# Two-layer transformer on one core: weights Hadamard-transformed by halves with sum and difference on leaving PSUM, and single-pass transposes of split keys and maxima

## The chip, the cores and the metric

The kernel runs on one core of a Trainium2 chip. The metric is the device time of one execution in microseconds (us), the median over several executions.

## The reference

The input x is 2 sequences of 1,024 rows of 256 numbers, all in float32. Two layers follow, each with attention and a feed-forward part that read the same normalised rows:

```python
xn = layernorm(x)
x = x + L0_attn(xn) + L0_ffn(xn)      # linear attention with elu+1; ternary weights
xn = layernorm(x)
x = x + L1_attn(xn) + L1_ffn(xn)      # softmax attention with rotary embedding; Hadamard FFN

# L1_ffn, with fwht the normalised Walsh-Hadamard transform over the last axis
h = fwht(xn * SU_ug) / 64
up, gate = h @ W_up.T * (Wscale_ug[:1024] * 64), h @ W_gate.T * (Wscale_ug[1024:] * 64)
y = fwht(silu(gate) * up * SU_dp) / 64
y = y @ W_down.T * (Wscale_dp * 64)
```

There are 16 heads of 16 numbers, and the inner width of the feed-forward parts is 1,024. The transforms act on the activations in the reference. The kernel moves them to the weights: it transforms the gate, up and down weights once and uses the transformed ("effective") weights in ordinary matrix products.

## The kernel before

Rows are kept in four chunks of 512. Products run on TensorE in float32, or, where operands are split into a high and a low part, in float32r (reduced float32), which TensorE takes in a single pass. PSUM is divided into two `pair` buffers for scores (two banks each), one bank `po` for attention outputs, and three `bank` buffers that everything else shares.

Up to about 290 us the kernel does layer 0 for the first sequence, the attention of layer 0 for the second, and a first search for maxima. From there on the softmax attention of layer 1 goes through eight units of four heads. A unit has 16 slots, and a slot has two halves. In each half TensorE makes a "burst": scores `scm` of the next unit, from which VectorE takes the maximum (`scores_max`, `peak`, L695), and scores `sce` of this unit minus their maxima, on which ScalarE takes the exponential (`weights_exp`, L740). In the first half TensorE then weighs the values (`weigh`, L748); in the second half it does other work that a planner hands out.

The order on the engines is written out by hand. Generators stand in the queue `filler` (the feed-forward part of layer 0, `hadamards`, `ffn1`), in `urgent` (`heads_of`, which makes the queries and keys of the next heads) and in `background` (`norm1` and `butterflies`). `slot` gives the filler its share, the work left (`left`) over the slots left (`to_fill`), and `fill` steps through the generators until their stated costs use the share up. A generator can also yield a mark: after SOON or FIRST it goes on after the burst of a first half, after SECOND after that of a second half (`go_on`). `fill` stops at FIRST and SECOND, and at SOON unless more than `LEAD` (0.85 us) of the share is unused. `background` is stepped once for each first half.

`hadamards` is

```python
yield from hadamard_down()            # ends with background.append(butterflies(wd1))
yield from hadamard_in("wgT1", "wA")
force(background)
yield from hadamard_in("wuT1", "wB")
```

`hadamard_in` transforms a weight of 256 x 1,024, held as two halves `raw[:, 0]` and `raw[:, 1]` of 128 rows. The 256-row transform is [[H, H], [H, -H]] with the 128-row matrix H (`hm`), so each of the two output halves is a sum of two products in PSUM; VectorE multiplies by the signs `su_ug` on the way out (L589). `butterflies` finishes the transform of the down weights in three levels of 1,024 columns, half on GpSimd (L614) and half on VectorE (L615), and then scales eight slices on VectorE (L619); its second buffer has the tag `wB`, which the effective up weights use afterwards. `force(background)` runs all that is left of `norm1(3)` and `butterflies` at once. `norm1` normalises a chunk (`norm_T`), transposes it and ends with the addition of the output bias to x on GpSimd (L438).

`heads_of` splits the rotated keys into a high and a low part (`split_k`), both written as float32r into `ks`; `lay_out` then transposes two groups of queries (float32, L475) and two of keys (L477) into a `bank` for each of eight row blocks. `put_peaks` transposes the negated maxima, also split into two float32r parts (`tops`), in four transposes (L719).

Of the kernel before, what the change touches and what calls it, by code (L numbers as in the profile page):

```python
# [20 lines left out]
P = 128  # L21
# [23 lines left out]
def tile_two_layers(ctx: ExitStack, tc: tile.TileContext, a: dict, out: bass.AP):  # L45
# [12 lines left out]
    def bank(name):  # L58
        return ps.tile([P, C], F32, tag="bank", name=name, bufs=3)
# [4 lines left out]
    def load(pool, name, view, shape, tag=None):  # L64
        tag, bufs = tag or (name, 1)
        t = pool.tile(list(shape), F32, tag=tag, name=name, bufs=bufs)
        nc.sync.dma_start(out=t, in_=view)
        return t
# [17 lines left out]

    ident = const.tile([P, P], F32, tag="ident", name="ident")
    make_identity(nc, ident)
    ones_r = const.tile([P, P], F32R, tag="ones_r", name="ones_r")
    nc.vector.tensor_scalar(ones_r, ident, 0.0, 1.0, ALU.mult, ALU.add)  # L90
    minus_half = const.tile([P, CT], F32, tag="minus_half", name="minus_half")
# [359 lines left out]
    def heads_of(b, gg, first=0, last=BT):  # L451

        if (b, gg) not in head_tiles:
            pool = late[0] if gg else at
            thk = pool.tile([P, 4, S], F32R, tag="qk_hi", name="qk_hi", bufs=1)
            tl = pool.tile([P, 2, S], F32R, tag="ql", name="ql", bufs=1)
            tv = pool.tile([P, BT, HH, VW], F32, tag="va", name="va", bufs=1)

            nc.gpsimd.memset(tv[:, :, :, HD:], 1.0)
            for i in range(2):  # L460
                g = 2 * gg + i
                qh[b, g], ql[b, g], kk[b, g] = thk[:, i, :], tl[:, i, :], thk[:, 2 + i, :]
                va[b, g] = tv[:, :, 4 * i : 4 * i + 4, :]
            head_tiles[b, gg] = thk, tl, tv
        thk, tl, tv = head_tiles[b, gg]
        half = HD // 2
        w3 = slice(gg * 3 * P, (gg + 1) * 3 * P)
        bias = qkvb[:, w3]

        def lay_out(i, rot, ks):  # L470
            cols = slice(i * P, (i + 1) * P)
            pt = bank("pt").rearrange("p (g n) -> p g n", g=4)
            for g in range(2):
                q4 = rot[:, 4 * g : 4 * g + 4, :, :].rearrange("p h s d -> p (h s d)")
                nc.tensor.transpose(pt[:, g, :], q4, ident)  # L475
                k4 = ks[:, 4 * g : 4 * g + 4, :, :].bitcast(F32).rearrange("p h s d -> p (h s d)")
                nc.tensor.transpose(pt[:, 2 + g, :], k4, ident)  # L477
            return cols, pt

        def take_out(cols, pt):  # L480
            nc.scalar.copy(thk[:, :, cols], pt)
            nc.vector.tensor_tensor(tl[:, :, cols], pt[:, 0:2, :], thk[:, 0:2, cols], ALU.subtract)

        def split_k(i):
            (rot,) = made[i]
            ks = at.tile([P, HH, 2, HD], F32R, tag="ks", name="ks")
            nc.scalar.copy(ks[:, :, 0, :], rot[:, HH:, 0, :])
            nc.gpsimd.tensor_tensor(ks[:, :, 1, :], rot[:, HH:, 1, :], ks[:, :, 0, :], ALU.subtract)
            made[i].append(ks)


        made = {}
        for i in range(first, last + 2):
            if i >= first + 2:
                cols, pt = lay_out(i - 2, *made.pop(i - 2))
                yield 4 * P * TR
                take_out(cols, pt)
            if i >= last:
                yield 0.0, LAST
                if i == last:  # L500
                    split_k(i - 1)
                    yield 0.0, PAIR
                continue
            c, j = divmod(b * BT + i, CT)
            pqkv = bank("pqkv")[:, 0 : 3 * P]
            for k in range(2):
                nc.tensor.matmul(  # L507
                    pqkv,
                    lhsT=xnT[c][:, k, j * P : (j + 1) * P],
                    rhs=wqkv[:, k, w3],  # L510
                    start=(k == 0),
                    stop=(k == 1),
                )
                if k == 0:
                    yield 3 * P * COL
            yield 3 * P * COL, LAST
            if i > first:
                split_k(i - 1)
            yield 0.0, FIRST
            qk = at.tile([P, 2 * HH, 2, half], F32, tag="qk", name="qk", bufs=1)  # L520
            nc.vector.tensor_add(qk.rearrange("p h t f -> p (h t f)"), pqkv[:, 0 : 2 * P], bias[:, 0 : 2 * P])
            nc.vector.tensor_add(
                tv[:, i, :, 0:HD],
                pqkv[:, 2 * P :].rearrange("p (h d) -> p h d", d=HD),
                bias[:, 2 * P :].rearrange("p (h d) -> p h d", d=HD),
            )
            cos, sin = (
                trig[:, i, s, :].unsqueeze(1).unsqueeze(1).to_broadcast([P, 2 * HH, 2, half]) for s in range(2)
            )
            qs = at.tile([P, 2 * HH, 2, half], F32, tag="qs", name="qs", bufs=1)  # L530
            nc.gpsimd.tensor_tensor(qs, qk, sin, ALU.mult)
            nc.gpsimd.tensor_tensor(qk, qk, cos, ALU.mult)

            rot = at.tile([P, 2 * HH, 2, HD], F32, tag="rot", name="rot")
            twice = [P, 2 * HH, 2, half]
            a0, a1, b0, b1 = (t[:, :, h, :].unsqueeze(2).to_broadcast(twice) for t in (qk, qs) for h in range(2))
            nc.gpsimd.tensor_tensor(rot[:, :, :, half:], a1, b0, ALU.add)
            yield 0.0, SECOND
            nc.vector.tensor_tensor(rot[:, :, :, 0:half], a0, b1, ALU.subtract)
            made[i] = [rot]  # L540
            yield 0.0, PAIR


    hm = load(const, "hadamard", a["hadamard"], [P, P])
    hneg = const.tile([P, P], F32, tag="hneg", name="hneg")
    nc.vector.tensor_scalar_mul(hneg, hm, -1.0)
    su_ug = load(const, "su_ug", a["su_ug"], [P, 2])
    su_dp = load(const, "su_dp", a["su_dp"], [P, NB])
    ws_dp = load_row(const, "ws_dp", D)

# [10 lines left out]
    def load_raw(count=2):  # L561
        for _ in range(count):
            if raws:
                name, n = raws.pop(0)
                raw = at.tile([P, 2, C], F32, tag="stage", name="raw", bufs=3)
                if name == "wdT1":
                    view = a[name].rearrange("(k p) n -> p k n", p=P)[:, 4 * n : 4 * n + 4, :]
                    nc.sync.dma_start(out=raw.rearrange("p a (b n) -> p (a b) n", b=2), in_=view)
                else:
                    view = a[name].rearrange("(k p) n -> p k n", p=P)[:, :, n * C : (n + 1) * C]  # L570
                    nc.sync.dma_start(out=raw, in_=view)
                loaded.append(raw)

    def hadamard_in(name, tag):
        eff = const.tile([P, 2, E], F32, tag=tag, name=f"eff_{name}")
        had[name] = eff
        for n in range(E // C):
            cols = slice(n * C, (n + 1) * C)
            raw = loaded.pop(0)
            for m in range(2):  # L580
                pw = bank("pw")
                for k, h in enumerate((hm, hneg if m else hm)):
                    nc.tensor.matmul(pw, lhsT=h, rhs=raw[:, k, :], start=(k == 0), stop=(k == 1))
                    if k == 0:
                        yield C * COL
                if m:
                    load_raw(1)
                yield C * COL, SOON
                nc.vector.tensor_scalar_mul(eff[:, m, cols], pw, su_ug[:, m : m + 1])  # L589
                yield 0.0  # L590

    def hadamard_down():
        wd1 = const.tile([P, NB, D], F32, tag="wC", name="wd1")
# [118 lines left out]
    def put_peaks(u, n):  # L712

        if n == 0:
            mx[u] = late[0].tile([P, S], F32R, tag="mx", name="mx")
        pt = bank("pt")
        for t in range(CT):
            top = tops[:, t, :, :].bitcast(F32).rearrange("p h d -> p (h d)")
            nc.tensor.transpose(pt[:, t * P : (t + 1) * P], top, ident)  # L719
        nc.scalar.copy(mx[u][:, n * C : (n + 1) * C], pt)  # L720
        left[0] -= CT * P * TR
        spent[0] += CT * P * TR

    def weights_of(u, i, p, sc):

# [140 lines left out]
    LEAD = 0.85  # L866
    ffn0_cost = 8 * NB * F * PASS + 2 * D * NB * 2 * PASS
    ffn1_cost = 48 * F * COL
    heads_cost = BT * (6 * P * COL + 4 * P * TR)
    norm_cost = 2 * CT * P * TR  # L870
    attention_cost = 2 * len(units) * norm_cost + NC * (norm_cost + CT * 2 * D * COL)

    with tc.manual_schedule(engines={PE}):

# [7 lines left out]
        def search(steps):  # L882
# [26 lines left out]
        filler += [*layer0[0:2], lambda: norm1(2), *layer0[2:4], lambda: norm1(3), hadamards()]  # L909
        filler += [ffn1(cc) for cc in range(8)]  # L910
        left[0] = (
            4 * ffn0_cost + 2 * norm_cost + 20 * C * COL + 8 * ffn1_cost + 3 * heads_cost + attention_cost
        )

    ordered[0] = True
# [125 lines left out]
```

## Time and profile before

| | |
|---|---|
| time, median of 3 runs | 970.14 us (968.78 to 972.83) |
| the profiled execution | 971.25 us, of which the span of the profile is 969.1 |
| mean granted TensorE clock | 0.974 |
| TensorE busy | 883.8 us, 91% of the span |
| VectorE, ScalarE, GpSimd busy | 586.2, 443.5, 215.4 us |
| transposes of keys (L477) and of maxima (L719) | 64 and 64 |
| matmul records of `pw` (all Hadamard products) | 40, between 400 and 441 us |

In the profile's lines a group is named by line, engine, operation and tiles (output<-inputs); then follow the count, the busy time in us and the mean duration in ns, and the idle time ahead of it with what ended it. In a timeline a line has the start, the length, the engine and the operation, and in brackets the idle time before it. A float32 product appears as two matmul records, a transpose or a float32r product as one.

### The profile page before, as it was taken

Reading aid. Unit: us, or ns where it says so; the run is one execution under the profiler, and the core shown is the slowest. Engines: PE = TensorE matmul, PEld = TensorE weight load, DVE = VectorE, ACT = ScalarE, POOL = GpSimd, SP = SyncE. Lnnn points to the kernel's source line nnn. Section 1 sums busy time; section 2 is a strip of 40 time slices with the busy share of each in tenths; the row PEclk is TensorE's granted clock in tenths of the full one; section 3 lists DMA queues with packets and bytes.
Section 4 is the critical chain, followed back from the end, with each engine's and each line's share of the span. In section 5 each row is a group of like instructions: output and inputs, shape, how many; then the busy total and the mean of one; then the engine's idle time right before and its main releaser. Section 6 shows DMA issues by size and latency. Waiting matters only on the chain.

```text
span 969.1 us, 14603 instructions
## 1 busy us (share of the span) xinstructions
PE 883.8 (91%) x6030; PEld 527.5 (54%) x6030; DVE 586.2 (60%) x975; ACT 443.5 (46%) x659; POOL 215.4 (22%) x287
## 2 busy tenths in 40 slices
PE   5778786878999999989999999999999999999987
PEld 2368674446555666434555555555555555555543
DVE  2744465478676687686775656567666665656311
ACT  5443435311454666334554434345444444444553
POOL 1634556510363233042420000045000000000000
PEclk9899898988899999999999999999999999999999
DMA  9100000000000001100000000000000000000000
GB/s 318 37 1 1 0 1 1 1 0 1 1 1 1 1 22 36 53 23 1 1 1 2 1 1 1 4 19 1 2 1 22 1 1 1 2 1 1 1 12 33
DMA packets 11249, 14.77 MB, mean 15 GB/s; under 512 B 1200, under 2 KB 8880, under 8 KB 11184
## 3 DMA queue, kind: packets, MB, share of 16 engines
q1 hardware_dynamic: 11184, 13.85, 4.3%
q8 instruction: 47, 0.77, 0.3%
q14 instruction: 18, 0.15, 0.0%
HBM read 11.75 MB, written 2.10 MB: 14 GB/s over the span
## 4 chain that ended last, share of the span: by engine, by line
PE 64%; DVE 23%; POOL 5%; issue 4%; ACT 3%; DMA 1%; SPq 0%; POOLq 0%; ACTq 0%; DVEq 0%
DVE peak L695 16%; PE scm L673 14%; PE pug L148 12%; PE sce L673 6%; PE py L171 6%; PE pqkv L507 4%; PE pug L96 4%; PE pkv L96 3%; PE py L96 2%; PE po L748 2%; POOL hid L385 2%; PE pq L96 1%; PE py L420 1%; PE sc L673 1%; ACT pr L740 1%
## 5 line engine op out<-in xcount | busy, mean ns | idle before, releaser
L740 ACT ACTIVATE pr<-sce 128x1024 f32<-128x1024 f32 x256 | 260.2, 1023 | 282.0 <-PE sce L673 281.8
L695 DVE TENSOR_REDUCE peak<-scm 128x2 f32<-128x1024 f32 x224 | 274.0, 1223 | 171.7 <-PE scm L673 170.6
L748 PE MATMUL po<-pr,va 128*17 128x512 f32 x1024 | 136.5, 602 | 0.0
L673 PE MATMUL scm<-qk_hi 32*128 32x512 f32 x448 | 112.2, 497 | 14.7 <-DVE peak L695 4.2
L673 PEld LDWEIGHTS scm<-qk_hi 32*128 32x128 f32 x448 | 41.7, 182 | 153.0 <-DVE peak L695 116.7
L673 PE MATMUL sce<-qk_hi 32*128 32x512 f32 x512 | 122.6, 497 | 2.6 <-ACT pr L740 1.8
L673 PE MATMUL sce<-mx,ones_r 32*128 32x512 f32 x512 | 97.1, 393 | 0.0
L673 PE MATMUL sce<-ql,qk_hi 32*128 32x512 f32 x512 | 97.0, 394 | 0.0
L709 POOL CAST tops<-nm 128x16 fp32r<-128x16 f32 x16 | 3.5, 219 | 388.6 <-DVE nm L698 388.5
L673 PE MATMUL scm<-qk_hi,ql 32*128 32x512 f32 x448 | 89.3, 395 | 0.0
L148 PE MATMUL pug<-xnT,eff_wgT 128*128 128x256 f32 x256 | 68.9, 391 | 0.1
L148 PE MATMUL pug<-xnT,eff_wuT 128*128 128x256 f32 x256 | 68.8, 383 | 0.0
L171 PE MATMUL py<-wd,hid 128*128 128x256 f32 x256 | 62.3, 388 | 0.0
L385 POOL TENSOR_TENSOR hid<-act,hid 128x256 fp32r<-128x256 f32 x64 | 46.8, 733 | 69.2 <-ACT hid L384 47.1
L171 PEld LDWEIGHTS py<-wd,hid 128*128 128x128 f32 x256 | 46.6, 190 | 16.2 <-issue 11.0
L158 ACT ACTIVATE act<-pug,ws_ug 128x256 f32<-128x256 f32 x64 | 30.3, 473 | 54.3 <-PE pug L148 54.3
L148 PEld LDWEIGHTS pug<-xnT,eff_wgT 128*128 128x128 f32 x256 | 46.0, 190 | 16.5 <-issue 10.3
L148 PEld LDWEIGHTS pug<-xnT,eff_wuT 128*128 128x128 f32 x256 | 47.8, 190 | 9.9 <-issue 3.3
L673 PEld LDWEIGHTS sce<-qk_hi 32*128 32x128 f32 x512 | 45.8, 182 | 11.9 <-ACT pr L740 8.2
L673 PEld LDWEIGHTS sce<-mx,ones_r 32*128 32x128 f32 x512 | 46.4, 184 | 10.5
L96 PE MATMUL pug<-xs,t_wuT 128*128 128x256 f32 x256 | 46.4, 304 | 4.7 <-DVE act L408 3.3
L507 PE MATMUL pqkv<-wqkvT,xnT 128*128 128x384 f32 x128 | 49.3, 506 | 0.9 <-DVE act L408 0.9
(157 smaller groups left out, 1349.0 us busy)
## 6 DMA issues: line engine op xcount, KB each, us to landing
x<-in_x SPq DMA_DIRECT2D x4, 512.0 KB, 7.7
out<-x SPq DMA_DIRECT2D x12, 128.0 KB, 1.7
both<-in_wuT SPq DMA_DIRECT2D x1, 1024.0 KB, 9.6
both<-in_wgT SPq DMA_DIRECT2D x1, 1024.0 KB, 11.7
wdT<-in_wdT SPq DMA_DIRECT2D x1, 1024.0 KB, 13.8
raw<-in_wdT SPq DMA_DIRECT2D x2, 512.0 KB, 3.4
raw<-in_wgT SPq DMA_DIRECT2D x2, 512.0 KB, 3.4
raw<-in_wuT SPq DMA_DIRECT2D x2, 512.0 KB, 3.4
```

The costliest lines, as they stand in the source:

```text
L96: nc.tensor.matmul(out_, lhsT=lhsT, rhs=rhs, start=(i == 0), stop=(i == len(pairs) - 1))
L148: nc.tensor.matmul(pug[:, w, :], lhsT=weight[:, k, cols], rhs=xnT[c][:, k, at : at + F], start=(k == 0), stop=(k == 1),)
L158: nc.scalar.activation(act, pug[:, 0, :], AF.Tanh, scale=half_scale(e))
L171: nc.tensor.matmul(py, lhsT=hid[e][:, cols], rhs=down[:, e, :], start=(e == 0), stop=(e == NB - 1))
L385: nc.gpsimd.tensor_tensor(h[1], act, h[0], ALU.subtract)
L420: nc.tensor.matmul(py, lhsT=hid[e][s][:, cols], rhs=wd[:, e, :], start=(e + s == 0), stop=(e + s == NB))
L507: nc.tensor.matmul(pqkv, lhsT=xnT[c][:, k, j * P : (j + 1) * P], rhs=wqkv[:, k, w3], start=(k == 0), stop=(k == 1),)
L673: nc.tensor.matmul(sc, lhsT=passes[s][0], rhs=passes[s][1], start=(s == 0), stop=(s == len(passes) - 1))
L695: nc.vector.tensor_reduce(peak[:, t, kh, 2 * p : 2 * p + 2], sc, AX.X, ALU.max, negate=True)
L709: nc.gpsimd.tensor_copy(tops[:, :, :, 0], nm)
L740: nc.scalar.activation(pr, sc, AF.Exp, scale=HD**-0.5)
L748: nc.tensor.matmul(po[h * HS : h * HS + VW, :], lhsT=va[b, g][:, kt, h, :], rhs=pr[h // 2][:, h % 2, :], start=(kt == 0), stop=(kt == BT - 1),
```

## The change

The effective gate and up weights are made in another way. Each raw half is multiplied by H once, into a `bank` of its own. ScalarE then writes the second product, times the signs, into SBUF, and VectorE adds the first product times the signs. This is done once for the sum (the first 128 output rows) and once, with the sign of the second product turned by `minus_su`, for the difference. The second pair of operations comes after a SECOND mark. The matrix `hneg` goes. Second, the keys and the maxima are transposed as the float32r values that they are, with an identity in float32r (`ident_r`), and not as float32. Third, the planner's sums of work are set to the new counts.

```diff
+    ident_r = const.tile([P, P], F32R, tag="ident_r", name="ident_r")
+    nc.vector.tensor_copy(ident_r, ident)
...
-                k4 = ks[:, 4 * g : 4 * g + 4, :, :].bitcast(F32).rearrange("p h s d -> p (h s d)")
-                nc.tensor.transpose(pt[:, 2 + g, :], k4, ident)
+                k4 = ks[:, 4 * g : 4 * g + 4, :, :].rearrange("p h s d -> p (h s d)")
+                nc.tensor.transpose(pt[:, 2 + g, :].bitcast(F32R), k4, ident_r)
...
-                yield 4 * P * TR
+                yield 3 * P * TR
...
-    hneg = const.tile([P, P], F32, tag="hneg", name="hneg")
-    nc.vector.tensor_scalar_mul(hneg, hm, -1.0)
     su_ug = load(const, "su_ug", a["su_ug"], [P, 2])
+    minus_su = const.tile([P, 1], F32, tag="minus_su", name="minus_su")
+    nc.vector.tensor_scalar_mul(minus_su, su_ug[:, 1:2], -1.0)
...
             raw = loaded.pop(0)
-            for m in range(2):
-                pw = bank("pw")
-                for k, h in enumerate((hm, hneg if m else hm)):
-                    nc.tensor.matmul(pw, lhsT=h, rhs=raw[:, k, :], start=(k == 0), stop=(k == 1))
-                    if k == 0:
-                        yield C * COL
-                if m:
-                    load_raw(1)
-                yield C * COL, SOON
-                nc.vector.tensor_scalar_mul(eff[:, m, cols], pw, su_ug[:, m : m + 1])
-                yield 0.0
+            pw = []
+            for k in range(2):
+                pw.append(bank("pw"))
+                mm(pw[k], [(hm, raw[:, k, :])])
+                if k == 0:
+                    yield C * COL
+            load_raw(1)
+            yield C * COL, SOON
+            nc.scalar.mul(eff[:, 1, cols], pw[1], su_ug[:, 0:1])
+            nc.vector.scalar_tensor_tensor(
+                eff[:, 0, cols], pw[0], su_ug[:, 0:1], eff[:, 1, cols], ALU.mult, ALU.add
+            )
+            yield 0.0, SECOND
+            nc.scalar.mul(eff[:, 1, cols], pw[1], minus_su)
+            nc.vector.scalar_tensor_tensor(
+                eff[:, 1, cols], pw[0], su_ug[:, 1:2], eff[:, 1, cols], ALU.mult, ALU.add
+            )
+            yield 0.0
...
-            top = tops[:, t, :, :].bitcast(F32).rearrange("p h d -> p (h d)")
-            nc.tensor.transpose(pt[:, t * P : (t + 1) * P], top, ident)
+            top = tops[:, t, :, :].rearrange("p h d -> p (h d)")
+            nc.tensor.transpose(pt[:, t * P : (t + 1) * P].bitcast(F32R), top, ident_r)
         nc.scalar.copy(mx[u][:, n * C : (n + 1) * C], pt)
-        left[0] -= CT * P * TR
-        spent[0] += CT * P * TR
+        left[0] -= CT * P * TR / 2
+        spent[0] += CT * P * TR / 2
...
-    heads_cost = BT * (6 * P * COL + 4 * P * TR)
+    heads_cost = BT * (6 * P * COL + 3 * P * TR)
...
-    attention_cost = 2 * len(units) * norm_cost + NC * (norm_cost + CT * 2 * D * COL)
+    attention_cost = 1.5 * len(units) * norm_cost + NC * (norm_cost + CT * 2 * D * COL)
...
-            4 * ffn0_cost + 2 * norm_cost + 20 * C * COL + 8 * ffn1_cost + 3 * heads_cost + attention_cost
+            4 * ffn0_cost + 2 * norm_cost + 12 * C * COL + 8 * ffn1_cost + 3 * heads_cost + attention_cost
```

## The prediction

> **What bounds the kernel now.** I read first the busy rows of the page and its slices, then the costliest groups, then the timelines of each engine around the place that is changed.
>
> ```profile
> PE 883.8 (91%) x6030; PEld 527.5 (54%) x6030; DVE 586.2 (60%) x975; ACT 443.5 (46%) x659; POOL 215.4 (22%) x287
> PE   5778786878999999989999999999999999999987
> L695 DVE TENSOR_REDUCE peak<-scm 128x2 f32<-128x1024 f32 x224 | 274.0, 1223 | 171.7 <-PE scm L673 170.6
> ```
>
> From slice 11 (about 290 us) on TensorE is full: the attention of layer 1 runs there in 120 slots of about 5.4 us, and the planner fills the second half of each slot with other matmuls ("filler"). A microsecond of filler taken away is a microsecond of time, as long as nobody makes TensorE wait. The one who does is VectorE: the next scores need the PSUM pair that `peak` (1.22 us) reads. In the timeline of TensorE one slot looks so:
>
> ```profile
> 408.65 0.50 PE L673 MATMUL scm<-qk_hi 32*128 32x512 f32 x2
> ...
> 409.54 1.05 PE L748 MATMUL po<-pr,va 128*17 128x512 f32 x8
> 410.70 0.50 PE L673 MATMUL scm<-qk_hi 32*128 32x512 f32 x2
> ...
> 411.68 1.13 PE L583 MATMUL pw<-raw,hadamard 128*128 128x512 f32 x2
> 412.64 1.02 PE L583 MATMUL pw<-raw,hneg 128*128 128x512 f32 x2
> 413.50 1.88 PE L583 MATMUL pw<-raw,hadamard 128*128 128x512 f32 x4
> 415.31 0.50 PE L673 MATMUL scm<-qk_hi 32*128 32x512 f32 x2
> ```
>
> The first half is 2.05 us (408.65 to 410.70), no longer than scores (0.75 to the last `scm`) plus `peak` (1.24): it has no slack for VectorE. The second half is scores (0.98) plus filler. The same stretch on VectorE and GpSimd already shows the danger:
>
> ```profile
> 425.41 1.22 DVE L695 TENSOR_REDUCE peak<-scm 128x2 f32<-128x1024 f32 x1
> 426.55 0.68 DVE L134 COPY xnT<-pt 128x512 f32<-128x512 f32 x1
> 427.14 3.62 DVE L619 SCALAR_TENSOR_TENSOR wd<-had_wd,su_dp,ws_dp 128x256 f32<-128x256 f32 x8
> 430.87 0.75 DVE L589 TENSOR_SCALAR eff_wuT<-pw,su_ug 128x512 f32<-128x512 f32 x1
> 431.54 1.22 DVE L695 TENSOR_REDUCE peak<-scm 128x2 f32<-128x1024 f32 x1
> ```
> ```profile
> 432.81 0.50 PE L673 MATMUL scm<-qk_hi 32*128 32x512 f32 x2 [1.65 <-DVE peak L695]
> ```
>
> The eight scalings of the down weights are issued at once by `force(background)`, the peak queues behind them, TensorE stands 1.65 us; with 1.08 us at 421.70 that is 2.7 us of stalls in this stretch.
>
> **What the Trainium skill says.** "FP8 and Floating Point Precision", TensorE Precision Notes: true FP32 takes four passes. The trace agrees: two 512-column products took 1.81 us (406.84 to 408.65), in records of 0.43 us, two to a product: 0.86 us, near 4 x 512 columns at 2.4 GHz. "TensorE: Matmul & The Clock Gate", Back-to-back issue gap: 134 cycles (56 ns) for 128 columns in one pass, but about 81 ns in a stream that reloads weights. No row here shows one pass of 128 columns; one pass of 256 takes 0.1175 us (four `pug` in 0.47 us), a little over the page's 262 cycles. Its section LDWEIGHTS gives P/1.2 ns, 107 ns for 128 columns. The trace agrees for ordinary loads: the one-column `pt<-part,ones_r` pair started 0.11 us apart. Same page, Architectural detail: VectorE and ScalarE are strict first-in first-out; the peak behind L619 above shows it.
>
> **The change, part by part.** *Hadamard matmuls.* `hadamard_in` issues 2 weights x 2 halves x 2 outputs x 2 = 16 products now; after, each raw half is transformed once: 8. Removed 8 x 0.86 = **6.9 us** of filler.
>
> *Sum and difference.* Removed: 8 VectorE TENSOR_SCALAR of 0.74 us. Added: 8 scalar_tensor_tensor of 512 columns (the 256-column ones take 0.415 to 0.484; I take 0.70, bounds 0.68 and 0.80) and 8 ScalarE multiplies (0.69, as L267 with its per-partition bias). VectorE's sum stays at 5.9 against 5.6; ScalarE's 5.5 us lie in its idle time (46% busy). But each VectorE step now waits for a ScalarE multiply, which is queued behind the `exp` (1.02 us) of its half slot, and the second pair comes a half slot later.
>
> *What is late next.* (a) A chunk holds two of three `bank` buffers until its second pair. The buffer freed first is taken first, so the next chunk's second product waits for the last multiply behind `exp`: burst start + 1.05 + 1.02 + 0.69 = 2.8, against 1.84 when TensorE wants it. About 0.9 us, twice. (b) `hadamard_in` of one weight now takes two slots, not four, so `force(background)` comes one or two slots sooner. `norm1(3)` and `butterflies` advance one step a slot. Laying out the queues by hand from the durations above: at the force the third butterfly level is still unissued, and it comes after `norm1(3)`'s bias addition (L438, 2.6 us) on GpSimd, 2.36 us itself; then the 3.6 us of scalings, then the multiply into `eff_wuT` (its buffer is the butterflies'), then the sum, and only then the peak. Beginning with the last `xn` at about 422: 422 + 2.6 + 2.4 + 3.6 + 0.7 + 0.7 + 1.2 = 433.2, while TensorE is ready at 426.7: **6.6 us** in place of 1.65. (c) In the same slot the last two `xn` (ScalarE) are queued behind `exp` and the second multiply, with `norm1`'s transposes waiting: 3.0 us. (d) Butterfly level one and the sums delay another peak: 1.3 + 0.4 + 0.7 us. Together 13.9 us. If the planner stands half a slot elsewhere, `xn` is made before the force and the butterfly a step further: 10.1 us by the same working. Net: 13.9 - 2.7 - 6.9 = +4.3 or 10.1 - 2.7 - 6.9 = +0.5; I take **+2.4 us**.
>
> *Transposes of keys.* 64 of them; now one per 0.109 us (L477 in steps of 0.11):
>
> ```profile
> L477 PE MATMUL pt<-ident,ks 128*128 128x128 f32 x64 | 16.2, 280 | 1.5 <-POOL ks L488 1.5
> L719 PE MATMUL pt<-ident,tops 128*128 128x128 f32 x64 | 10.5, 287 | 0.0
> ```
>
> One pass: at best 0.056, at worst the ordinary load, 0.1175 (dearer than now); the transposes' load records are 0.14 us against 0.19, so transposes load faster than products, and I take 0.056. For keys even the slow load is covered by the neighbouring FP32 transpose of q. In the slots: 48 x 0.053 = 2.5 us; 16 lie before 290 us, where TensorE is not full: half of 0.8, 0.4 us. *Maxima*: 64 in rows of four, 4 of them while others wait: 60 x 0.053 = 3.2 us at best, 60 x -0.008 = -0.5 at worst. Together **-6.1 us** (worst: -1.9).
>
> *At nothing*: `ident_r` (0.2 us on VectorE, hidden under the first load of x), `minus_su` for `hneg` (1.28 us less on VectorE at 35.7 us, where TensorE waits for other things), and the planner's sums: they hand 12.8 us less filler to 120 slots, 0.1 us each, out of about 2.5. Uncovered these would cost at most 0.3 us. No DMA is added or moved; `load_raw` stays between the same products.
>
> Sum: +2.4 - 6.1 = -3.7. The profiled execution took 971.25 (span 969.1 and 2.15 around it), 1.1 above the median 970.14: 967.5 in its terms, **966.4** against the median.
>
> **Rivals.** *The waits don't bite (0.25)*: the background is further on than I laid out, stalls stay near 3 to 5 us; -6.9 + 1.5 - 6.1 = -11.5, 958.6. For it: TensorE's stalls in the stretch are only 2.7 us now. Against: the force comes earlier by construction. *Single-pass transposes are load-bound (0.19)*: +2.4 - 1.9 = +0.5, about 970.6. For it: 256-column products in one pass already take 0.1175, not 0.109. Against: the short load records of transposes. *Slower (0.11)*: the forced butterfly blocks the peak even longer. If GpSimd's third level slips a further slot behind, stalls reach 17 us and with load-bound transposes 17 - 2.7 - 6.9 - 1.9 = +5.5: 975.6. It decides once the stalls of the stretch exceed 2.7 + 6.9 plus what the transposes save, 15.7 us if those are fast, 11.5 if not. *The change not doing what it says (0.03)*: a reduced-precision transpose run in as many passes as FP32; then about +2.
>
> **How the numbers follow.** My forecast (0.42) spans 962 to 969. A measurement of this kernel tells 0.5% (4.85 us) from none. Below 965.3: the first rival (0.25), some 0.18 of the forecast, 0.02 of the others: 0.45. Above 975: 0.10. Between: 0.45. The range from 957.5 to 973 leaves out less than 2 in 10.
>
> **What would show it.** Right: 16 records of `pw` for 32, `ks` and `tops` transposes in steps of 0.056, a peak that ends 3 us or more behind `wd` L619, TensorE idle of 4 us or more once before `scm` between 410 and 440 us. Wrong: no TensorE wait above 2 us in that stretch (then 959), or `tops` in steps of 0.11 (then 970).

## The result, and the profile after

The changed kernel takes **986.36 us** (median of 4 runs, 983.77 to 986.98), against 970.7 us of the kernel before on the same chip: a ratio of 1.0156, with a 95% interval of 1.0127 to 1.0184. It is slower by some 15 us, where 966.4 was forecast and 973 was the upper end. The profiled execution took 986.31 us, with a span of 984.3 us, against 971.25 and 969.1. In the profile after, lines stand 2 to 10 further down: `peak` is L705, `scm` and `sce` L683, `tops` L729, `ks` L479, the first butterflies L624 and L625.

These rows of the page after answer to those shown of before; the row of granted clock is added.

```profile
PE 886.9 (90%) x6014; PEld 525.0 (53%) x6014; DVE 588.1 (60%) x976; ACT 448.5 (46%) x667; POOL 216.8 (22%) x287
PE   5778776888898999969999999999999999999987
PEclk9899887988899999988999999999999999999999
L705 DVE TENSOR_REDUCE peak<-scm 128x2 f32<-128x1024 f32 x224 | 274.1, 1223 | 165.2 <-PE scm L683 164.0
```

The same row of before:

```profile
PEclk9899898988899999999999999999999999999999
```

TensorE has 16 instructions less and still 3.1 us more of busy time (886.9 against 883.8): matmuls took longer where the clock was halved. Its idle time grew from 85.3 (969.1 - 883.8) to 97.4 us. Slices are 24.6 us. Counted from zero, the clock is lower than before in slices 5 and 6 (123 to 172 us, 8 and 7 for 9 and 8), where nothing of the weights' transform runs, and in 17 and 18 (418 to 468 us, 8 for 9), where it does. The rows of transposed maxima serve as marks: the first starts at 241.04 us before and at 250.24 after, so **9.2 us** are lost ahead of the slots. The stretch in which the weights are transformed, between two later rows of that kind, takes 61.6 us (401.95 to 463.58) in place of 49.5 (394.10 to 443.62), **12.1 us** more. Some 6 us of that come back in the other slots, where there is now less filler to do.

The stretch after, on TensorE (columns: start, length, engine, line, operation; in brackets the idle time and who ended it):

```profile
422.40 1.13 PE L98 MATMUL pw<-raw,hadamard 128*128 128x512 f32 x2 [0.64 <-ACT eff_wgT L596]
...
429.84 0.33 PE L131 MATMUL pt<-ident,xn 128*128 128x128 f32 x1 [2.15 <-ACT xn L122]
430.33 0.33 PE L131 MATMUL pt<-ident,xn 128*128 128x128 f32 x1 [0.16 <-ACT xn L122]
432.30 1.82 PE L131 MATMUL pt<-ident,xn 128*128 128x128 f32 x6 [1.65 <-ACT xn L122]
433.92 3.62 PE L98 MATMUL pw<-raw,hadamard 128*128 128x512 f32 x4
...
442.94 0.79 PE L683 MATMUL sce<-qk_hi 32*128 32x512 f32 x2 [2.50 <-DVE peak L705]
```

GpSimd and then VectorE in the same place:

```profile
432.82 2.35 POOL L440 TENSOR_TENSOR x<-x,ob 128x1024 f32<-128x1024 f32 x1 [3.69 <-ACT xn L122]
435.13 3.34 POOL L624 TENSOR_TENSOR had_wd<-wd 128x1024 f32<-128x1024 f32 x1
```
```profile
438.50 3.26 DVE L629 SCALAR_TENSOR_TENSOR wd<-had_wd,su_dp,ws_dp 128x256 f32<-128x256 f32 x8 [2.25 <-POOL had_wd L624]
441.67 1.22 DVE L705 TENSOR_REDUCE peak<-scm 128x2 f32<-128x1024 f32 x1
```

This is the predicted chain: late `xn`, the bias addition to x, the last butterfly, the scalings, and only then the maximum that the scores wait for. (The multiply into `eff_wuT` and the sum, which the prediction put ahead of this maximum, come behind it here.) What was not predicted is in the lengths on TensorE. Four `pw` records took 1.88 us before and take 3.62 here, and first `sce` pairs 0.79 in place of 0.50. The table by stretches (start:end, length, busy us of PE, PEld, DVE, ACT and POOL, granted clock, DMA share, GB/s) says why:

```profile
425.00:430.00 5.00, 2.85 (x27) 1.11 (x21) 4.14 (x5) 2.42 (x4) 4.05 (x2) 1.00 0.02 3
430.00:435.00 5.00, 3.18 (x10) 2.01 (x10) 3.01 (x5) 3.33 (x6) 2.18 (x1) 0.65 0.00 0
435.00:440.00 5.00, 4.86 (x23) 1.45 (x22) 2.75 (x5) 1.02 (x1) 3.46 (x2) 0.66 0.01 2
440.00:445.00 5.00, 2.50 (x11) 1.44 (x12) 4.75 (x8) 1.05 (x2) 0.00 (x0) 0.68 0.00 0
445.00:450.00 5.00, 5.00 (x22) 1.26 (x21) 1.65 (x4) 2.49 (x4) 0.00 (x0) 0.64 0.00 0
```

With each of the two long waits the clock fell to half, from 431.5 and from 441.8 us on, for 6.8 us each time. In the kernel before, all stretches from 420 to 450 us have a clock of 1.00. Over the whole profile the time lost to a lower clock (one minus the clock, summed over stretches of 2 us) is 38 us after and 26 us before.

### The profile page after: what moved, and what is told of

The parts are those of the page before. It is cut to its first block, busy times and chain, and to the rows that moved or that the text cites. A ratio compares the mean times of both kernels' runs of the same rounds, so it can differ in the third digit from the quotient of the medians.

```text
span 984.3 us, 14574 instructions
## 1 busy us (share of the span) xinstructions
PE 886.9 (90%) x6014; PEld 525.0 (53%) x6014; DVE 588.1 (60%) x976; ACT 448.5 (46%) x667; POOL 216.8 (22%) x287
## 4 chain that ended last, share of the span: by engine, by line
PE 62%; DVE 22%; POOL 6%; issue 5%; ACT 4%; DMA 1%; SPq 0%; POOLq 0%; ACTq 0%; DVEq 0%
DVE peak L705 16%; PE scm L683 14%; PE pug L150 12%; PE sce L683 6%; PE py L173 6%; PE pqkv L509 4%; PE pug L98 4%; PE pkv L98 3%; PE py L98 2%; POOL hid L387 2%; PE pq L98 2%; PE po L758 2%; ACT pr L750 1%; PE py L422 1%; PE sc L683 1%
## 5 line engine op out<-in xcount | busy, mean ns | idle before, releaser
L705 DVE TENSOR_REDUCE peak<-scm 128x2 f32<-128x1024 f32 x224 | 274.1, 1223 | 165.2 <-PE scm L683 164.0
L683 PE MATMUL sce<-qk_hi 32*128 32x512 f32 x512 | 123.6, 498 | 5.7 <-DVE peak L705 3.8
L683 PE MATMUL scm<-qk_hi 32*128 32x512 f32 x448 | 112.3, 498 | 13.5 <-DVE peak L705 2.6
L683 PEld LDWEIGHTS scm<-qk_hi 32*128 32x128 f32 x448 | 41.6, 183 | 151.5 <-DVE peak L705 114.1
L683 PE MATMUL sce<-ql,qk_hi 32*128 32x512 f32 x512 | 97.2, 393 | 0.0
L683 PE MATMUL sce<-mx,ones_r 32*128 32x512 f32 x512 | 96.9, 390 | 0.0
L683 PE MATMUL scm<-qk_hi,ql 32*128 32x512 f32 x448 | 89.6, 397 | 0.0
L683 PEld LDWEIGHTS sce<-qk_hi 32*128 32x128 f32 x512 | 46.0, 183 | 16.3 <-ACT pr L750 8.8
L683 PEld LDWEIGHTS sce<-mx,ones_r 32*128 32x128 f32 x512 | 46.6, 184 | 10.8
## 6 DMA issues: line engine op xcount, KB each, us to landing
both<-in_wgT SPq DMA_DIRECT2D x1, 1024.0 KB, 11.9
```

The costliest lines, as they stand in the source:

```text
L683: nc.tensor.matmul(sc, lhsT=passes[s][0], rhs=passes[s][1], start=(s == 0), stop=(s == len(passes) - 1))
L705: nc.vector.tensor_reduce(peak[:, t, kh, 2 * p : 2 * p + 2], sc, AX.X, ALU.max, negate=True)
```

## The experiments

The theory after the result was that each of the three parts has its own share, and that the stated costs, which issue no instruction, have the largest. The rivals were that the Hadamard stalls alone are larger than predicted, or that the single-pass transposes are dear. Except where stated, an edit is made to the kernel before.

**e1_order_only**: the stated cost of `lay_out`, and nothing else. Every instruction of the kernel before is kept. (The sum `heads_cost` stays at 4 here and in e8 and e11; the changed kernel sets it to 3 as well. So the slots of these runs are not dealt out quite as in the changed kernel.)

```diff
-                yield 4 * P * TR
+                yield 3 * P * TR
```

> The kernel before, with one number changed: the cost that lay_out states for its four transposes, 3 in place of 4. No instruction is changed, only the order in which weave deals out the work before 290 us (and the fill of the slots that heads_of shares). Theory (the new order costs the prologue 9 us, not the new transposes): the first transpose of maxima moves from 241 to 250 us and the whole takes 976 to 981. Rival (single-pass transposes among FP32 ones stall TensorE or throttle its clock): first maxima within 1 us of 241, the whole within 2 us of before.

Measured: 988.25 us (984.92 to 990.69), ratio 1.0177 (1.0149 to 1.0206). One number that a generator tells its planner makes a loss as large as the whole one. The theory had only half of it (976 to 981): the first maxima come at 247.37 us, 6.3 us late, and the slots lose the rest. TensorE has the same 6030 instructions and is busy longer:

```profile
PE 895.7 (91%) x6030; PEld 532.9 (54%) x6030; DVE 588.3 (60%) x975; ACT 443.9 (45%) x659; POOL 214.1 (22%) x287
```

Of the 15.6 us on the span, 11.9 are busy time (895.7 - 883.8) and 3.7 idle. The time lost to a lower clock is 36 us, 10 more than before. Lined up against the kernel before, the order of TensorE's instructions parts first at the interleaving of layer 0 with the first heads: a row of 26 `py` is cut into 20, then `pqkv` and transposes, then 12 with the rest, and projections `pqkv` that were issued in twos now come singly; in the slots, among other shifts, a pair of `pug` moves one slot forward. The table by stretches, kernel before first:

```profile
130.00:140.00 10.00, 7.03 (x50) 6.23 (x51) 6.71 (x20) 5.08 (x13) 7.09 (x10) 1.00 0.00 0
140.00:150.00 10.00, 7.23 (x46) 5.68 (x44) 5.64 (x21) 3.43 (x9) 7.58 (x10) 1.00 0.00 0
150.00:160.00 10.00, 5.50 (x28) 3.92 (x29) 5.06 (x9) 6.83 (x15) 8.56 (x8) 0.66 0.01 2
160.00:170.00 10.00, 9.08 (x42) 4.58 (x41) 6.62 (x8) 5.17 (x9) 4.74 (x4) 1.00 0.00 0
```
```profile
130.00:140.00 10.00, 8.04 (x40) 6.60 (x40) 5.30 (x15) 3.71 (x9) 5.96 (x9) 0.83 0.00 0
140.00:150.00 10.00, 7.13 (x37) 6.02 (x37) 4.71 (x12) 3.31 (x8) 3.81 (x7) 0.83 0.00 0
150.00:160.00 10.00, 4.28 (x23) 2.74 (x21) 4.64 (x14) 2.47 (x6) 7.53 (x10) 0.76 0.01 2
160.00:170.00 10.00, 9.22 (x32) 4.85 (x36) 4.17 (x5) 7.04 (x15) 8.23 (x4) 0.56 0.00 1
```

From 130 to 150 us TensorE is about as busy as before or busier and issues 77 matmuls where it issued 96. The changed kernel shows the same picture in these 40 us: 0.83, 0.83, 0.75 and 0.56. Not all of it comes from the order: the half clock of the first row begins at 131.3 us, ahead of the first difference in order (137 us), after a wait of 1.98 us that the kernel before has too (1.96, with the clock kept). The runs e3, e4, e6, e9, e10 and e11 have a drop there as well and reach the first maxima at 239 to 242 us, so this one costs little. The wait of 2.40 us at 142 us and the half clock from 155.2 to 168.8 us come after the order has parted.

**e2_transposes_only**: the two kinds of transposes in one pass, the stated costs left as they were. To make room for `ident_r`, one small buffer for statistics is kept three times instead of four.

```diff
+    ident_r = const.tile([P, P], F32R, tag="ident_r", name="ident_r")
+    nc.vector.tensor_copy(ident_r, ident)
-                nc.tensor.transpose(pt[:, 2 + g, :], k4, ident)
+                nc.tensor.transpose(pt[:, 2 + g, :].bitcast(F32R), k4, ident_r)
-            nc.tensor.transpose(pt[:, t * P : (t + 1) * P], top, ident)
+            nc.tensor.transpose(pt[:, t * P : (t + 1) * P].bitcast(F32R), top, ident_r)
```

> The kernel before with the single-pass transposes alone: every stated cost and sum of the planner as before, the Hadamard part as before (one small statistics buffer has three copies for four, to make room). Theory (single-pass transposes are cheaper by themselves): 963 to 966, first maxima at 240 to 241 us. Rival (they cost the prologue its 9 us): 972 or more. Second rival (bound by the load of weights): 968 to 970.

Measured: 970.47 us (968.29 to 976.12), ratio 0.9999 (0.9985 to 1.0012): no gain that can be told. A row of maxima in the kernel before and in this one:

```profile
394.10 0.66 PE L719 MATMUL pt<-ident,tops 128*128 128x128 f32 x4
394.59 0.27 PE L764 MATMUL pt<-ident,oT 128*128 128x128 f32 x1
```
```profile
396.67 0.53 PE L721 MATMUL pt<-ident_r,tops 128*128 128x128 f32 x4
397.04 0.62 PE L766 MATMUL pt<-ident,oT 128*128 128x128 f32 x4
```

From the first of four transposes to the next instruction it takes 0.37 us in place of 0.49. That is 0.12 x 16 = 1.9 us in the whole kernel. The keys gain too: from the first of a block's four transposes (q, key, q, key) to the next instruction it takes 0.397 us in place of 0.493 (medians of the trace), 3.1 us in 32 blocks. Less than half of this shows: from the first row of maxima to the last this profile takes 663.6 us, the kernel before 665.2. And ahead of the first row it is 2.9 us later, with a lower clock. The profiled execution, 972.69 us at a clock of 0.970, is not typical: 13 of the 20 have a clock of 0.972 or more, as all of the kernel before beside them have, and their median is 969.5 us, 2.0 below the 971.45 of that kernel. The other seven, at 0.967 to 0.970, take 972.7 to 976.1. So a small gain is likely, and it is smaller than what the clock moves.

**e3_after_cost4**: the changed kernel with the one number set back.

```diff
-                yield 3 * P * TR
+                yield 4 * P * TR
```

> The kernel after, with the cost that lay_out states put back to 4. Theory: the prologue is as it was before, first maxima near 241 us, and the whole drops from 986 to 976 to 979, the rest of the loss lying in the Hadamard stretch. Rival (the loss of the prologue comes from the transposes): 985 to 987.

Measured: 973.8 us (969.83 to 981.43), ratio 1.0033 (1.0016 to 1.0051). Setting it back takes 12.6 us from the changed kernel, more than the theory had. It starts its first row of maxima at 240.66 us, where the changed one does at 250.24.

**e4_hadamard_only**: the new `hadamard_in` with `minus_su` and the sum's 12 for 20, the rest as before.

> The kernel before with the new hadamard_in alone (and its sum in the planner, 12 for 20). Theory (earlier force: transposes of norm1 wait for xn, GpSimd's last butterfly comes after the bias addition, scalings hold up the peak, and the idle TensorE falls to a lower clock): stalls above 10 us between 405 and 445, granted clock below 0.8 for some 15 us there, the whole 976 to 981. Rival (the stretch alone is about even, as forecast): 971 to 974. Rival (half the products gone is a gain): 963 to 966.

Measured: 972.9 us (970.8 to 975.07), ratio 1.0015 (1.0006 to 1.0025), some 1.5 us. The changed weights alone cost little, as forecast; the theory of 976 to 981 fell. The stalls between 405 and 445 us add up to 9 us, and the clock is at half from 432.0 to 438.9 us, once and not twice as in the changed kernel. The stretch between the two rows of maxima takes 55.7 us with 9.6 idle; in the changed kernel it takes 61.6 with the same 9.6 idle.

**e7_cost3_prologue** and **e8_cost3_slots**: e1 in two halves, the number 3 for the heads ahead of the slots only, or for those in the slots only.

```diff
-                yield 4 * P * TR
+                yield (3 if (b, gg) == (0, 0) else 4) * P * TR    # e7; e8 has 3 and 4 exchanged
```

> The kernel before, with the cost 3 for 4 in lay_out for the first two heads alone (made before 290 us by weave). Theory (the order of the prologue costs 6 us there and nothing later): first maxima at 246 to 250, the whole 976 to 979. Rival (the state that the prologue leaves shifts the slots as well, and the whole loss of 17 us hangs on it): 985 to 989.

> The kernel before, with the cost 3 for 4 in lay_out for the later heads alone (made in the slots from 290 us). Theory (the slots hand out 0.1 us more filler eight times a unit, which shifts where the filler waits for GpSimd's hid and lets the clock fall): first maxima at 241, the whole 976 to 981, with drops of the clock between 300 and 450 that before does not have. Rival (it is the prologue alone): 970 to 972.

Measured: e7 979.82 us (977.14 to 983.56), ratio 1.0098 (1.0066 to 1.0131); e8 979.74 (978.65 to 980.9), ratio 1.0095 (1.0080 to 1.0110). Each half costs about 9 us, and together they make e1's 17. In e7's profile the loss lies ahead of the slots: first maxima at 253.70 us, 12.7 late, and the span 12.6 longer (of an execution that took 983.56 us). In e8 the first maxima come at 241.34 us, and the loss lies behind them. One of the places reads so:

```profile
329.90 0.64 PE L420 MATMUL py<-t_wdT,hid 128*128 128x256 f32 x2 [0.24 <-POOL hid L385]
331.84 0.56 PE L420 MATMUL py<-t_wdT,hid 128*128 128x256 f32 x1 [1.29 <-POOL hid L385]
332.32 0.79 PE L673 MATMUL scm<-qk_hi 32*128 32x512 f32 x2
...
333.90 1.72 PE L748 MATMUL po<-pr,va 128*17 128x512 f32 x8
335.56 0.49 PE L673 MATMUL scm<-qk_hi 32*128 32x512 f32 x2
```

`py` is asked for before GpSimd has written its `hid`: a wait of 1.29 us, and after it 3.4 us at half clock (0.79 for 0.50, 1.72 for 1.05). The kernel before waits 1.36 us for a `hid` at 335.37 us and keeps its clock there. Two more drops follow in e8 that it does not have, behind waits of 1.23 us (365.18) and 3.51 us (434.55).

**e11_cost5**: the number set the other way.

```diff
-                yield 4 * P * TR
+                yield 5 * P * TR
```

> The kernel before, with the stated cost of lay_out at 5 in place of 4, no instruction changed. Theory (the order dealt out at 4 happens to suit the waits, and any other number shifts it): a change of 3 us or more in either direction, likelier slower, 974 to 988. Rival (a lower stated cost packs the heads too close and a higher one relaxes them): 966 to 970.

Measured: 971.11 us (969.17 to 975.05), ratio 1.0004 (0.9988 to 1.0020). No difference, so it is not so that any other order is worse: the theory fell. The number 3 deals a bad order, the number 5 a good one. Why 3 and not 5 stays open; no run singles out the first wait that tips it. The clock moves this kernel too: its four executions of 969.2 to 970.3 us have a granted clock of 0.975 to 0.977, its five above 974 one of 0.968 to 0.972.

**e5_hadamard_drained** and **e6_hadamard_reversed**: e4 with another end of `background`. In e5 the queue is waited for, step by step, ahead of the force; in e6 the butterflies go ahead of the bias addition.

```diff
+        while background:            # e5
+            yield 0.0, FIRST
+        background.reverse()         # e6, instead of it
         force(background)
```

> The kernel before with the new hadamard_in, and background drained one step a slot ahead of the force, so that nothing is left to force; the filler gives these slots nothing. Theory (the forced rest of norm1 and butterflies is what the new Hadamard part pays with): no TensorE idle stretch above 2 us and no clock below 0.9 between 405 and 450 us; 965 to 968, four to seven below the Hadamard part alone (972.9). Rival (the waits of the sums behind the exponentials and the held PSUM buffers are what costs): 971 to 973. The empty slots themselves should cost 1 us each, 3 to 5 of them.

> The kernel before with the new hadamard_in, and the force taking butterflies ahead of norm1, so that GpSimd's last level is not behind the bias addition. Theory (GpSimd's order makes some 2.5 us of the peak's delay): the long wait of scm for the peak shrinks by 2 to 3 us, 969 to 971. Rival (the scalings of 3.6 us on VectorE alone make it, or they now hold up the copy of xnT): 972 to 974.

Measured: e5 975.0 us (974.34 to 975.71), ratio 1.0046 (1.0031 to 1.0061), against 1.0015 for e4; e6 971.07 (968.59 to 975.32), ratio 1.0005 (0.9989 to 1.0020). In e6 the last butterfly does go ahead (421.09 us, the bias addition at 423.41), but the wait that this was to shorten stays: 4.71 us, where e4 has 4.81. The scalings, with the bias addition now beside them on GpSimd, take 5.20 us and not 3.26. In e4 the scalings start when VectorE's own half of the last butterfly ends (428.47 us); that of GpSimd ended at 427.38. First e4, then e6:

```profile
428.56 3.26 DVE L627 SCALAR_TENSOR_TENSOR wd<-had_wd,su_dp,ws_dp 128x256 f32<-128x256 f32 x8
```
```profile
424.62 5.20 DVE L627 SCALAR_TENSOR_TENSOR wd<-had_wd,su_dp,ws_dp 128x256 f32<-128x256 f32 x8
431.59 0.79 PE L682 MATMUL scm<-qk_hi 32*128 32x512 f32 x2 [4.71 <-ACT pr L749]
```

So e6's theory fell, although the time came out beside its range: the medians differ by 1.8 us, the ratios by 0.1%, and their intervals overlap. In e5 the theory fell as well. While the queue drains, TensorE waits for maxima 1.30 us at 420.13, 0.89 at 427.14 and 2.17 at 440.21, and the clock stays at half for 13.6 us (419.8 to 433.5) though TensorE is busy again:

```profile
420.00:425.00 5.00, 4.87 (x26) 2.10 (x30) 3.19 (x4) 2.09 (x3) 1.45 (x1) 0.50 0.00 0
425.00:430.00 5.00, 4.11 (x25) 2.21 (x21) 2.45 (x2) 1.90 (x2) 0.00 (x0) 0.50 0.00 0
```

But over the whole profile e5 loses 31 us to a lower clock, no more than e4. What makes it slower than e4 is not shown.

**e10_hadamard_warm**: e4 with six products whose result is not used, into a spare `bank`, issued where TensorE waits for the forced work.

```diff
         force(background)
+        warm[0] = 6
...
                             weigh(*pending.pop(0))
+                        if warm[0]:
+                            spare = bank("pt")
+                            for _ in range(warm[0]):
+                                nc.tensor.matmul(spare, lhsT=ident, rhs=xnT[0][:, 0, :], start=True, stop=True)
+                            warm[0] = 0
```

> The new hadamard_in alone, with six products added whose results nobody reads (5.2 us), after the weighing of the slot that follows the force, where TensorE waits for the peak. Theory (the stall costs its length and then a half clock for 7 us, 3.4 us lost): the drop at 432 to 439 us goes, 969 to 970.5 against 972.9 without. Rival (the wait alone counts): 972.5 to 974.

Measured: 971.07 us (967.61 to 976.17), ratio 1.0003 (0.9991 to 1.0014), 1.8 us below e4 by medians, 1.2 by the ratios, whose intervals overlap. It lies between the ranges of the theory and of the rival. First e4, then e10:

```profile
433.59 0.79 PE L681 MATMUL scm<-qk_hi 32*128 32x512 f32 x2 [4.81 <-ACT pr L748]
...
436.17 2.08 PE L96 MATMUL pw<-raw,hadamard 128*128 128x512 f32 x2
```
```profile
429.04 5.42 PE L967 MATMUL pt<-xnT,ident 128*128 128x512 f32 x12
434.39 0.50 PE L684 MATMUL scm<-qk_hi 32*128 32x512 f32 x2
...
435.81 1.12 PE L96 MATMUL pw<-raw,hadamard 128*128 128x512 f32 x2
```

The work came 0.8 us later behind the extra products, and then ran at full speed: two `pw` records in 1.12 us in place of 2.08. The 22 executions have a median clock of 0.972, those of e4 0.968. So filling the wait removed the half clock; that the halved clock is a cost of its own beside the wait is likely, but a gain in time of this size is not clear of the noise.

**e9_warm_prologue**: the kernel before with four such products ahead of its longest wait (5.41 us at 153 us).

```diff
+            if (b, gg, last, i) == (0, 0, CT, CT - 1):
+                for _ in range(4):
+                    nc.tensor.matmul(raw, lhsT=ident, rhs=xnT[0][:, 0, :], start=True, stop=True)
```

> The kernel before, with four products added whose results nobody reads (0.86 us each, into the PSUM buffer that the next transposes overwrite), where TensorE waits 5.4 us for GpSimd's rot at 147.7 us. Theory (an idle stretch of TensorE brings its clock to one half for some 4 to 7 us, and that is what a small wait costs): no drop of the clock between 150 and 160 us, 2 to 4 us less in all, 967 to 969. Rival (the clock falls for other reasons, or the drop is hidden by waits for other engines): 970 to 972.

Measured: 971.43 us (968.92 to 973.41), ratio 0.9993 (0.9977 to 1.0008): no difference. Two waits are left behind the filled one:

```profile
154.12 0.33 PE L479 MATMUL pt<-ident,rot 128*128 128x128 f32 x1 [1.96 <-POOL rot L541]
...
157.39 0.80 PE L677 MATMUL sc<-qk_hi 32*128 32x512 f32 x4 [1.86 <-ACT qk_hi L485]
```

The half clock came some 3 us later and stayed as long (155.4 to 162.2 us, before 151.9 to 158.7); the lost clock time is 25 us against 26. The theory fell here.

**e12_combination**: the transposes of e2 with the old stated costs, the weights as in e6, and extra products in the places of e9 and e10 and at two more waits of the part ahead of the slots.

> Single-pass transposes at the old stated costs, the new hadamard_in with butterflies ahead of norm1 in the force, and products that nobody reads in four idle stretches (two of state0, the one of rot, the one after the force). If idle stretches cost by the clock, 960 to 966; if not, 969 to 972.

Measured: 970.37 us (967.55 to 975.95), ratio 0.9996 (0.9979 to 1.0014). It equals the kernel before and does not beat it. This is not a full test, for in the profile the products after the force came too late, behind the wait and at half clock:

```profile
433.39 6.23 PE L978 MATMUL pt<-xnT,ident 128*128 128x512 f32 x8 [3.58 <-DVE xnT L136]
```

Their wait is put down to the copy from a `bank` to `xnT` on VectorE, which stands behind the scalings once the butterflies go first. And a higher clock alone is no gain here: the median clock of its executions is 0.977, that of the kernel before beside them 0.973, and the times are the same. (The profiled execution took 975.95 us at 0.972.)

## Why the prediction was wrong, point by point

*What bounds the kernel.* Right as far as it went (slice 11, counted from one, begins at 242 us; 290 us is where slice 13 begins). It left out the clock of TensorE. The kernel before has 26 us of lost clock time in it, and the reorderings of e1 and of the changed kernel raised that to 36 and 38.

*"At nothing: the planner's sums."* **This is the step that failed.** It priced the stated costs by the filler that they hand out in the slots, "at most 0.3 us", and said nothing of the 3 for 4 that `lay_out` yields. But a stated cost also sets the order in which the work is dealt, ahead of the slots too. e1, which changes this one number, costs 17 us; e7 and e8 show that both halves of the program suffer. In the changed kernel, setting it back (e3) wins 12.6 of the 15 us. How a changed order turns into time, by waits and by the clock behind them, is read from the traces and not tested apart.

*The Hadamard part.* +2.4 us forecast, +1.5 measured in e4. The chain was right, its sizes were not, and that the net came out nearly as said is partly luck. In the changed kernel the transposes waited 2.15 + 0.16 + 1.65 = 4.0 us for `xn` (3.0 in the working). From there to the end of the peak it took 10.6 us (432.30 to 442.89; the working had 11.2, from 422 to 433.2, with the multiply and the sum in it), with the last butterfly at 3.34 us for 2.36. But the scores waited only 2.50 us for that peak, where 6.6 was said: TensorE itself was ready 8.1 us after the last `xn` (432.30 to 440.44), where the working had 4.7, with most of that time at half clock. In e4 the one long wait is 4.81 us. The second product of a weight waited 0.64 us (0.9 was said). TensorE's idle time in the stretch rose from 3.4 us (49.52 - 46.08 busy) to 9.6 (61.63 - 52.05), by 6.1, a little under the +7.4 and +11.2 of the working's two cases. The half clock after the waits, which was not in the working, probably makes up for part of what the waits fell short.

*The transposes.* -6.1 us forecast, nothing that can be told in e2. The mis-sized term is 0.056 us for one pass of 128 columns: in a row of maxima four and the next start take 0.37 us, so about 0.09 each. They are 1.9 us cheaper for all maxima where 3.2 was said. Of the two figures in the Trainium skill's "TensorE: Matmul & The Clock Gate", Back-to-back issue gap, the nearer one here is that for a stream that reloads weights, about 81 ns; I chose the 56 ns of the isolated gap. The keys came out nearly as said, 0.048 us each (half of 0.493 - 0.397) for 0.053. So some 5 us of TensorE's time were saved, and at most 2 of them show in e2's time; what took the rest is open. The rival of load-bound transposes was nearer in its sum of -1.9, by luck: it put a transpose at 0.1175 us. (That -1.9 is also too small by its own terms, -2.5 - 0.4 + 0.5 = -2.4. And the two `pt<-part,ones_r` records started 0.03 us apart, not 0.11; it is the weight loads beside them that started 0.11 us apart.)

*The rival on the slow side* had the wrong mechanism. It asked for stalls of the forced butterfly above 11.5 us; the idle time of the whole stretch is 9.6 us, and the loss came mostly from an order that no rival treated. Of the signs named, the 16 `pw` records came; the steps of `tops` were 0.08 to 0.09 us, neither 0.056 nor 0.11; and in the changed kernel no wait before scores reached 4 us.

*The sum of parts.* 17 (e1) + 1.5 (e4) + 0 (e2) = 19 us against 15 measured; they do not simply add up. Between the first maxima and 402 us the changed kernel loses nothing (151.7 us, before 153.1), where e8 loses 6.0 us up to the same row; and its Hadamard stretch is 5.9 us longer than e4's, all of it busy time (52.05 against 46.19), with a granted clock of 0.89 for 0.94. How the loss divides is open.

## What to carry to other kernels

A number that feeds a planner is an edit to the instruction order: try it alone, with the instructions untouched, before crediting or blaming the instructions that came with it. When a kernel is full on TensorE, a new wait can cost twice, by its length and by the slower clock behind it, so look at the granted clock by stretches before and after. Filling waits with unused products did not make this kernel faster (e9, e12). Where a price may be an isolated or a sustained figure, take the sustained one for instructions that each load their own weights.

## What was not expected of the hardware

The granted clock falls to 0.5 with shorter waits than I thought: 1.29 us (behind another of 0.24) in e8, 1.30 (behind 0.82) in e5, 2.15 (with 0.16 and 1.65 behind it) in the changed kernel. It then stays low for 3.4 us or a multiple of it, in e5 for 13.6 us. The Trainium skill ("TensorE: Matmul & The Clock Gate", Part 1: The HAM clock gate) describes a window of some 3.4 us that runs freely and halves the clock when it is found idle; the length of the drops agrees. But the page's advice to avoid gaps above about 3 us (Why this matters for your kernels) is too mild for this kernel.

A wait doesn't always bring it about: in the kernel before one of 1.36 us at 304.75 us was followed by a drop, and one of 1.36 us at 335.37 us was not. The traces show what goes with a drop. In each of the fourteen, every fall of the clock lies on one grid of 3.41 us. Between 35 and 955 us the clock falls 161 times from full to half, always after a grid interval in which TensorE was busy for no more than 67% of the time. It never stays full after one that was busy for less than 45%; in between it does either. So the place of a wait on the grid counts as well as its length. The wait of 1.65 us at 432.81 us in the kernel before is divided by a grid line (431.8 us): the two intervals are busy for 82% and 70%, and the clock stays full. In e11 the interval that ends at 432.7 us is busy for 47%, and the clock falls. This reading is of busy shares beside clocks, not an experiment. That filling a wait removed a drop in e10 supports it; in e9 filling one of several only moved the drop.
